# Splitting the pole transforms ahead of a spectral layer: half of the channels ahead, the rest in four parts inside the loop

## The chip, the core and the metric

The kernel runs on one core of a Trainium2 chip. Time is the device time of that core in microseconds (us). The engines are named as in the profile: PE is TensorE (matmul; PEld its weight loads), DVE is VectorE, ACT is ScalarE, POOL is GpSimd, and SP is the engine from whose queue most DMAs are issued. Each engine takes its instructions in a fixed order and waits on semaphores for the others. A smaller time is better.

## What is computed

The reference passes x of 16 x 16 x 256 x 256 through four residual layers, each `x = x + layer(group_norm(x))`: a 3x3 convolution written with FFTs, a filter of 5 taps on the diagonal, a Laplace layer with poles and residues, and a quantised 3x3 convolution. The change lies at the start of the third, layer 2:

```python
alpha = fft2(x)
A  = 1.0 / (omega1[:, None, None, None] - weights_pole1[None])   # [y, i, k, p]
Bm = 1.0 / (omega2[:, None, None, None] - weights_pole2[None])   # [x, i, k, q]
S = einsum('ikpq,oikp,xikq->oxik', weights_residue, A, Bm)
output_residue1 = einsum('biox,oxik->bkox', alpha, S)            # then ifft2
C = einsum('biox,oikp->bikpx', alpha, A)
D = einsum('bikpx,xikq->bikpq', C, Bm)
output_residue2 = einsum('bikpq,ikpq->bkpq', D, weights_residue)
```

There are 16 input channels i, 16 output channels k and 4 poles on each axis. C and D are not taken from alpha in the kernel: A and Bm are transformed back to the image domain once ("hats"), and then multiplied with x there.

## The kernel before

Layers 0 and 1 run together over the 16 samples and write their result to the DRAM tensors `x2d`. At their end the group statistics of the last sample come in, and then layer 2's first stage begins, in three pieces:

- *Tables.* `table(...)` loads constants: `y1`, `x1`, `x2`, `m1`, `m2`, `not0` to stay, and `full`, `nat`, `diag` for the pole transforms.
- *Pole transforms* (lines 699 to 731). For each axis m of two, the 1024 poles (16 channels of 64) are loaded, real part `pr` and imaginary part `pi`, each broadcast to all 128 partitions (L706, L707). For two halves o of the frequencies: `g = (pi - w)^2` and `e = pi - w` on ACT (L716, L717), `g + pr^2` and its reciprocal on DVE (L719), then `im = e g` on POOL, `nre = pr g` on DVE and `re = -nre` on ACT (L722). Sixteen pairs of matmuls with `full` then give `hats[m]` for all channels (L729), in groups that ACT copies out of PSUM (L731). An fp32 matmul appears as two records of PE in the profile. After this `rt`, the residues on a diagonal, is made (two products on DVE).
- *The loop*, 128 steps n: four groups of four samples, in each group eight pairs of channels, in each pair four samples b. `quarters` loads x and forms sums and differences (`u`, `qd`, on DVE and POOL). `forth` does, per channel, the transform along y and the product with `hats[0]` on PE (L766, L769) into one of three `ps_y` buffers, and ACT copies it out as `y` (L771). `across` does the transform along x (L780) into two of three `ps_a` buffers, ACT copies one (`pc`, L785), DVE makes `al` (L787, L788), and PE multiplies with `hats[1]` (L796), which DVE weighs with `rt` and POOL sums. `project` runs for each sample at the end of its channels (L813). Channels 8 to 15 of the hats are first needed at step n = 16, channels 12 to 15 at n = 24.

Beside the loop runs side work for the next stage, the generator `aside`: `sums_over_q` (L577 to L630), then `poles(0)` and `masked(0, 0)`. It is cut into 56 pieces, and `next(aside, None)` at the end of a step emits one.

Order: inside the loop PE is in the order in which the code is written (`manual_schedule` of PE alone). The order of the other engines, and all orders ahead of the loop, are set by a scheduler, so that side work can stand well ahead of the step in which it is written. The tiles of the pole transforms lie in the pool `tp`, which is given back before the loop; the pool `head` holds `af0`, `af1` and `l00` to `l11`, which `poles` and `masked` use later.

## Time and profile before

| | us |
|---|---|
| median of 3 runs (4469.8 to 4476.33) | 4475.6 |
| the profiled execution | 4466.67 |
| its span | 4464.9 |
| first table load for layer 2 issued | 1283.41 |
| first matmul of the loop (L766) | 1367.24 |
| last copy of y in the loop (L771), start | 2250.0 |

Times inside the span count from its start. PE is busy 89% of the span, PEld 69%, DVE 68%, ACT 62%, POOL 49%. In a timeline row the first number is the start, the second the length of the merged instructions, and what stands in brackets is the idle time of the engine before it and what ended that. In a row by groups the numbers after the count are the busy time and the mean nanoseconds of one instruction, then the idle time before. In a row by stretch each engine has its busy time and its number of instructions, and the last three columns are the granted PE clock (1.00 is full), the busy share of the DMA engines and GB/s.

### The profile page before, as it was taken

Reading aid. Unit: us, or ns where it says so; the run is one execution under the profiler, and the core shown is the slowest. Engines: PE = TensorE matmul, PEld = TensorE weight load, DVE = VectorE, ACT = ScalarE, POOL = GpSimd, SP = SyncE. Lnnn points to the kernel's source line nnn. Section 1 sums busy time; section 2 is a strip of 40 time slices with the busy share of each in tenths; the row PEclk is TensorE's granted clock in tenths of the full one; section 3 lists DMA queues with packets and bytes.
Section 4 is the critical chain, followed back from the end, with each engine's and each line's share of the span. In section 5 each row is a group of like instructions: output and inputs, shape, how many; then the busy total and the mean of one; then the engine's idle time right before and its main releaser. Section 6 shows DMA issues by size and latency. Waiting matters only on the chain. (4 is left out here: it accounts for less than half of the span.)

```text
span 4464.9 us, 122570 instructions
## 1 busy us (share of the span) xinstructions
PE 3986.4 (89%) x50800; PEld 3069.6 (69%) x50800; DVE 3051.8 (68%) x5654; ACT 2752.2 (62%) x3667; POOL 2208.0 (49%) x3466
## 2 busy tenths in 40 slices
PE   4999999999948999899989999997999999995776
PEld 1555555555527999899967777775778888883444
DVE  4767676767677878787755555554566666767998
ACT  2877777777623444444458888887544444445998
POOL 2242424232345546464556666664677777773222
PEclk9999999999978999999989999998999999997999
DMA  6777776767443545354447777777887878876998
GB/s 144 166 174 168 168 174 163 179 158 183 105 113 103 164 136 172 123 162 153 152 101 166 164 170 166 167 172 173 219 219 219 219 217 230 235 205 240 350 351 310
DMA packets 431340, 820.54 MB, mean 184 GB/s; under 512 B 41600, under 2 KB 306816, under 8 KB 415360
## 3 DMA queue, kind: packets, MB, share of 16 engines
q1 hardware_dynamic: 365248, 577.52, 50.2%
q0 software_dynamic: 65536, 235.18, 16.8%
q8 instruction: 401, 6.57, 0.7%
q14 instruction: 155, 1.27, 0.1%
HBM read 408.85 MB, written 336.07 MB: 167 GB/s over the span
## 5 line engine op out<-in xcount | busy, mean ns | idle before, releaser
L382 PE MATMUL ps<-va,wt 128*64 128x512 f32 (+1 forms) x1632 | 668.9, 571 | 11.4 <-POOL va L354 9.2
L382 PE MATMUL ps<-vb,wt 128*64 128x512 f32 (+1 forms) x1632 | 667.1, 570 | 4.6 <-DMA vb<-va 4.6
L878 ACT COPY sk<-ps_s 64x516 f32<-64x516 f32 x1016 | 593.0, 584 | 117.8 <-PE ps_s L873 98.5
L771 ACT ACTIVATE y<-ps_y,bc 128x384 f32<-128x384 f32 x512 | 297.1, 581 | 423.1 <-PE ps_y L769 423.1
L873 PE MATMUL ps_s<-t,l 128*128 128x258 f32 x2048 | 523.5, 398 | 18.7 <-ACT sk L878 8.1
L190 DVE TENSOR_TENSOR ob<-ps_m,other 128x256 f32<-128x256 f32 x512 | 271.1, 607 | 355.5 <-ACT other L966 350.8
L403 ACT ACTIVATE v<-xt,nm 32x2048 f32<-32x2048 f32 x248 | 497.2, 2005 | 9.8 <-PE ps L417 3.5
L417 PE MATMUL ps<-v,w1s 128*64 128x259 f32 x4096 | 481.8, 395 | 11.0 <-DVE v L401 6.7
L382 PEld LDWEIGHTS ps<-va,wt 128*64 128x64 f32 x1632 | 223.3, 137 | 311.3 <-issue 282.8
L873 PEld LDWEIGHTS ps_s<-t,l 128*128 128x128 f32 x2048 | 372.2, 192 | 93.5 <-ACT sk L878 8.4
L417 PEld LDWEIGHTS ps<-v,w1s 128*64 128x64 f32 x4096 | 337.2, 141 | 133.0 <-issue 24.1
L1079 PE MATMUL ps_o<-exp,fs 128*128 128x128 f32 x2048 | 402.7, 279 | 14.2 <-ACT fs L1125 14.2
L1078 PE MATMUL ps_o<-c_last,zt 128*128 128x128 f32 x2048 | 401.7, 278 | 0.2
L1218 PE MATMUL ps_c<-q,wt 64*64 64x512 bf16 (+1 forms) x4608 | 288.1, 401 | 105.2 <-ACT o L1265 88.1
L1078 PEld LDWEIGHTS ps_o<-c_last,zt 128*128 128x128 f32 x2048 | 327.1, 195 | 63.1 <-issue 62.5
L941 PEld LDWEIGHTS ps_m<-z,sk 128*32 128x32 f32 x16384 | 254.5, 110 | 129.3 <-issue 108.3
L941 PE MATMUL ps_m<-z,sk 128*32 128x64 f32 x16384 | 303.7, 222 | 38.6 <-issue 35.3
L190 POOL TENSOR_TENSOR acc<-acc,prod 128x256 f32<-128x256 f32 x240 | 228.2, 951 | 216.0 <-DVE prod L190 209.3
L190 POOL TENSOR_TENSOR w<-rq 128x512 f32<-128x512 f32 x256 | 320.9, 1280 | 26.2 <-ACT rq L1080 15.4
L1079 PEld LDWEIGHTS ps_o<-exp,fs 128*128 128x128 f32 x2048 | 317.0, 195 | 15.4 <-ACT fs L1125 15.4
L1218 PEld LDWEIGHTS <-wt 64*64 64x64 bf16 x4800 | 179.8, 113 | 213.8 <-issue 144.7
L766 PE MATMUL ps_y<-c_y,qd 128*128 128x128 f32 x2048 | 315.9, 277 | 5.1 <-ACT y L771 5.1
(347 smaller groups left out, 8853.0 us busy)
## 6 DMA issues: line engine op xcount, KB each, us to landing
xt<-x2d SPq DMA_DIRECT2D x256, 512.0 KB, 4.3
z<-alphad SPq DMA_DIRECT2D x516, 129.0 KB, 4.8
xt<-in_x_dram SPq DMA_DIRECT2D x256, 256.0 KB, 7.2
x2d<-x2s POOLq DMA_DIRECT2D x256, 256.0 KB, 5.0
mixd<-ob SPq DMA_DIRECT2D x128, 512.0 KB, 5.8
ot<-mixd SPq DMA_DIRECT2D x256, 256.0 KB, 7.2
x3d<-xt POOLq DMA_DIRECT2D x128, 512.0 KB, 5.7
xt<-x3d SPq DMA_DIRECT2D x64, 1024.0 KB, 8.8
```

The lines of the kernel that those rows point to most:

```text
L190: eng.tensor_tensor(o, a, b, op)
L382: nc.tensor.matmul(ps[halves[h], lo:hi, :], lhsT=wt0[:, w, :], rhs=v[:, 2 * t + lo : 2 * t + hi, j : j + N], start=j == 0 and k == 0, stop ...
L403: nc.scalar.activation(to, o.xt[c][q_], AF.Identity, bias=o.g.nm[q_, 1:2])
L417: nc.tensor.matmul(ps[halves[h], k, 0:U], lhsT=o.w1[:, w : w + 64], rhs=v1[:, lo : lo + U], start=first_, stop=not first_)
L766: nc.tensor.matmul(to[:, :, a, :], lhsT=v[:, c, a, i % 2, :], start=a == 0, stop=a == 1, rhs=y1[:, a].rearrange("p (r f) -> p r f", r=2))
L771: nc.scalar.activation(y[:, c, :], ps[:, 0 : 3 * P], AF.Copy, scale=bc2[:, b, i // 2, 0:1])
L873: nc.tensor.matmul(ps[:, d, 0 : 2 * NX], lhsT=ls[h][:, k + d - k0], rhs=t2[:, h, k + d].rearrange("p x r -> p (x r)"), start=True, stop=True)
L878: copy(sks[2 * e8 + n][64 * h : 64 * h + 64, :, 2 * k : 2 * k + 4] .rearrange("p x (k r) -> p x k r", r=2), ps[64 * n : 64 * n + 64, :, 0 ...
L941: nc.tensor.matmul(to, lhsT=sk[:, x_], rhs=z[:, :, x_], start=True, stop=True)
L1078: nc.tensor.matmul(ps[:, a, c, :], lhsT=zts[d][:, a, c, :], rhs=last[:, c, :], start=True, stop=False)
L1079: nc.tensor.matmul(ps[:, a, c, :], lhsT=fs[:, d, a, :], rhs=ey[:, d, c, :], start=False, stop=True)
L1218: nc.tensor.matmul(o, lhsT=wt[half[h], w, :], rhs=src, start=i == 0, stop=i == len(work[0]) - 1)
```

## The change

The pole transforms become a function `transforms(m, i0, ni, pool)` for `ni` channels from `i0`. It is called for channels 0 to 7 of both axes ahead of the loop, and four times inside it, for four channels each, after the matmuls of steps 2, 4, 8 and 10 (axis 0 and then axis 1 for channels 8 to 11, axis 1 and then axis 0 for channels 12 to 15). Inside the loop its tiles are those of `head`; `full` stays for the whole stage; the tile `cf` of the side work moves to `head`'s `af1`. e and g have one buffer each, where there was one for each half o. The side work begins at n = 17 in place of 9 and is dense from n = 61 in place of 81.

```diff
-        cf = new(pool, [HC * C, 4, NP], "cf")
+        cf = (new(head, [HC, 2, C, FC], "af1").rearrange("p h r k f -> p (h r k f)")
+              .rearrange("p (n m q) -> p n m q", m=4, q=NP))
...
-            full = table(tp, "full").rearrange("p (h m f) -> p h m f", m=2, h=2)
+            full = table(wp, "full").rearrange("p (h m f) -> p h m f", m=2, h=2)
             nat, diag = table(tp, "nat"), table(tp, "diag")
-            for m, (t, pole) in enumerate(((ty, p1b), (tx, p2b))):
+            ws = []
+            for m, t in enumerate((ty, tx)):
                 rs = over_step(tp, t, f"b{m}")
...
+            def transforms(m, i0, ni, pool):
+                pole, n = (p1b, p2b)[m], ni * KP
+                if pool:
+                    pr, pi, h, e, g = (pool.tile([P, n], F32, tag=k, name=f"{k}{m}") for k in ("pr", "pi", "h", "e", "g"))
+                    re, im, nre = (pool.tile([P, 2, n], F32, tag=k, name=f"{k}{m}") for k in ("re", "im", "nre"))
+                else:
+                    ts = [new(head, [2, n], k) for k in ("l00", "l10", "l01", "l11", "af0", "af1")]
+                    pr, pi, h, e, g = ts[0][:, 0], ts[0][:, 1], ts[1][:, 0], ts[1][:, 1], ts[2][:, 0]
+                    re, im, nre = ts[3:]
+                at = slice(i0 * KP, i0 * KP + n)
+                nc.sync.dma_start(pr, pole[0:1, at].to_broadcast([P, n]))
+                nc.sync.dma_start(pi, pole[1:2, at].to_broadcast([P, n]))
                 tt(Q, h, pr, pr, MUL)
                 for o in range(2):
-                    e, g = (tp.tile([P, C * KP], F32, tag=f"{k}{o}", name=f"{k}{m}{o}") for k in ("e", "g"))
-                    nc.scalar.activation(g, pi, AF.Square, bias=nw[:, o : o + 1])
-                    nc.scalar.activation(e, pi, AF.Identity, bias=nw[:, o : o + 1])
+                    nc.scalar.activation(g, pi, AF.Square, bias=ws[m][:, o : o + 1])
+                    nc.scalar.activation(e, pi, AF.Identity, bias=ws[m][:, o : o + 1])
                     tt(V, g, g, h, ADD)
                     V.reciprocal(g, g)
                     tt(Q, im[:, o, :], e, g, MUL)
                     tt(V, nre[:, o, :], pr, g, MUL)
                     nc.scalar.mul(re[:, o, :], nre[:, o, :], -1.0)
+                nb = min(ni, 8)
                 for o in range(2):
-                    for i in range(0, C, 8):
-                        cols = slice(i * KP, (i + 8) * KP)
+                    for i in range(0, ni, nb):
+                        cols = slice(i * KP, (i + nb) * KP)
                         for r, parts_ in enumerate(((re, im), (im, nre))):
                             ps = ps_y.tile([P, 8, KP], F32, tag="ps_y", name="ps_hat")
+                            to = ps[:, 0:nb]
...
-                            nc.scalar.copy(hats[m][:, o, i : i + 8, r, :], ps)
+                            nc.scalar.copy(hats[m][:, o, i0 + i : i0 + i + nb, r, :], to)
+
+            for m in range(2):
+                transforms(m, 0, 8, tp)
...
-            if n > 7 and (n % 2 or n > 80):
+            if n in (2, 4, 8, 10):
+                transforms(n // 2 % 2 ^ 1, 8 + 4 * (n > 7), 4, None)
+            if n > 15 and (n % 2 or n > 60):
                 next(aside, None)
```

More of the change, by code (lines that the diff above doesn't have):

```diff
@@ L698, in layers @@
             tp = tmp.enter_context(tc.tile_pool(name="b_t", bufs=1))
-            full = table(tp, "full").rearrange("p (h m f) -> p h m f", m=2, h=2)
+            full = table(wp, "full").rearrange("p (h m f) -> p h m f", m=2, h=2)
             nat, diag = table(tp, "nat"), table(tp, "diag")
-            for m, (t, pole) in enumerate(((ty, p1b), (tx, p2b))):
+            ws = []
+            for m, t in enumerate((ty, tx)):
                 rs = over_step(tp, t, f"b{m}")
-                w = tp.tile([P, 2], F32, tag=f"wn{m}", name=f"wn{m}")
+                w, nw = (wp.tile([P, 2], F32, tag=f"{k}{m}", name=f"{k}{m}") for k in ("wn", "nw"))
@@ L704, in layers @@
                 V.tensor_scalar(w, nat, rs, TWO_PI, MUL, MUL)
-                pr, pi, h = (tp.tile([P, C * KP], F32, tag=k, name=f"{k}{m}") for k in ("pr", "pi", "h"))
-                nc.sync.dma_start(pr, pole[0:1, :].to_broadcast([P, C * KP]))
-                nc.sync.dma_start(pi, pole[1:2, :].to_broadcast([P, C * KP]))
-                re, im, nre = (tp.tile([P, 2, C * KP], F32, tag=k, name=f"{k}{m}") for k in
-                               ("re", "im", "nre"))
-                nw = tp.tile([P, 2], F32, tag=f"nw{m}", name=f"nw{m}")
@@ L712, in layers @@
-                V.tensor_scalar(nw, w, -1.0, None, MUL)
+                V.tensor_scalar(nw, w, -1.0, None, MUL)
+                ws.append(nw)
+            def transforms(m, i0, ni, pool):
[10 more added lines that the diff above has]
+                nc.sync.dma_start(pi, pole[1:2, at].to_broadcast([P, n]))
@@ L722, in layers @@
                     nc.scalar.mul(re[:, o, :], nre[:, o, :], -1.0)
+                nb = min(ni, 8)
                 for o in range(2):
-                    for i in range(0, C, 8):
-                        cols = slice(i * KP, (i + 8) * KP)
+                    for i in range(0, ni, nb):
+                        cols = slice(i * KP, (i + nb) * KP)
                         for r, parts_ in enumerate(((re, im), (im, nre))):
                             ps = ps_y.tile([P, 8, KP], F32, tag="ps_y", name="ps_hat")
+                            to = ps[:, 0:nb]
                             for k, v_ in enumerate(parts_):
-                                nc.tensor.matmul(ps.rearrange("p i k -> p (i k)"), lhsT=full[:, o, k],
+                                nc.tensor.matmul(to.rearrange("p i k -> p (i k)"), lhsT=full[:, o, k],
                                                  rhs=v_[:, o, cols], start=k == 0, stop=k == 1)
-                            nc.scalar.copy(hats[m][:, o, i : i + 8, r, :], ps)
+                            nc.scalar.copy(hats[m][:, o, i0 + i : i0 + i + nb, r, :], to)
+            for m in range(2):
+                transforms(m, 0, 8, tp)
             res = tp.tile([P, 2, C, NP], F32, tag="res", name="res")
```

## The prediction

> **What bounds the kernel now.** I read the page first, then busy time by stretch around the place of the change, then the waits and the timeline of that place, and last the loop that follows it.

> ```profile
> span 4464.9 us, 122570 instructions
> PE 3986.4 (89%) x50800; PEld 3069.6 (69%) x50800; DVE 3051.8 (68%) x5654; ACT 2752.2 (62%) x3667; POOL 2208.0 (49%) x3466
> ```

> TensorE (PE) fills 89% of the span, so a gain has to come from a place where it stands still. Busy time by stretch (columns: stretch, length, busy time and instructions of each engine, granted clock, DMA):

> ```profile
> 1292.00:1313.00 21.00, 0.16 (x1) 0.16 (x1) 17.58 (x16) 6.62 (x7) 6.29 (x3) 0.50 0.62 182
> 1313.00:1330.00 17.00, 16.09 (x31) 6.85 (x32) 17.00 (x9) 7.90 (x11) 9.97 (x5) 0.84 0.29 93
> 1330.00:1351.00 21.00, 0.95 (x3) 0.15 (x1) 21.00 (x9) 1.64 (x2) 6.83 (x4) 0.63 0.18 50
> 1351.00:1367.00 16.00, 16.00 (x32) 6.97 (x33) 5.57 (x6) 5.16 (x8) 2.51 (x2) 0.84 0.21 66
> 1427.00:1477.00 50.00, 50.00 (x450) 50.00 (x449) 39.22 (x74) 22.80 (x49) 28.50 (x29) 1.00 0.53 170
> ```

> Between layer 1 and the loop of layer 2 the third number, VectorE (DVE), is full (17 of 17, 21 of 21) while PE has nothing or runs pole transforms. In the loop (last row) PE is full and DVE has 10.8 of 50 us free. The timeline of that place (start, length, engine, line, operation):

> ```profile
> 1283.41 0.35 SPq L186 DMA_DIRECT2D c_mod<-in_const_dram  x1
> ...
> 1297.34 1.22 DVE L190 TENSOR_TENSOR g<-g,h 128x1024 f32<-128x1024 f32 x1
> ...
> 1300.81 6.54 DVE L719 RECIPROCAL g<-g 128x1024 f32<-128x1024 f32 x1
> ...
> 1308.35 3.35 DVE L190 TENSOR_TENSOR nre<-pr,g 128x1024 f32<-128x1024 f32 x1
> ...
> 1348.49 4.44 DVE L190 TENSOR_TENSOR nre<-pr,g 128x1024 f32<-128x1024 f32 x2
> 1350.85 2.07 PE L729 MATMUL ps_hat<-re,c_full 128*128 128x512 f32 x2 [20.05 <-ACT re L722]
> ...
> 1367.24 0.61 PE L766 MATMUL ps_y<-c_y,qd 128*128 128x128 f32 x4
> ```

> The chain is: tables and poles load, DVE works from 1297.3 to 1352.9, PE does the last 32 transform records, and at 1367.24 the loop begins. Then the loop itself; first the copies of y, which are four in a step, so 32 are eight steps, then two of its instructions with the idle time before them, a sum of waits, and a row of the side work:

> ```profile
> 1368.20:1426.70 58.50, 18.50 (x32) 0.94 0.35 107
> 1426.70:1476.80 50.10, 18.61 (x32) 1.00 0.53 169
> ```
> ```profile
> 1389.64 0.63 ACT L604 ACTIVATE qg<-qe 128x516 f32<-128x516 f32 x1 [8.39 <-POOL qe L190]
> 1390.79 1.22 PE L766 MATMUL ps_y<-c_y,qd 128*128 128x128 f32 x4 [5.07 <-ACT y L771]
> ```
> ```profile
> PE ps_a L780 <- DVE al L788: 10.3, 9, 2.5
> L607 DVE RECIPROCAL qg<-qg 128x516 f32<-128x516 f32 x8 | 27.0, 3378 | 16.9 <-POOL qg L190 16.9
> ```

> A step takes 50.1/8 = 6.26 us, all PE. The first eight take 58.5; step 0 lacks one `across` (1.34, from its first record at 1370.70 to the next matmul at 1372.04), so they are 58.5 - 48.7 = 9.8 over. About 8 of it is one PE wait of 5.07, because ScalarE (ACT) stood 8.39 us at a Square of the side work with the copies of y queued behind it, and slow records in the step after (9.11 us from copy to copy, 2.85 over).

> **The change, part by part.** Each part is costed against the profiled execution (4466.67 us, 8.9 under the median of the runs, 4475.6). 0.2%, about what a measurement of this kernel can tell from no change, is 9 us.

> (1) *The stretch ahead.* DVE from the first addition to the last nre: 1352.93 - 1297.34 = 55.6 us without idle time. Four reciprocals are 26.2; the other 29.4 are four additions, four nre and two rt of 1024, four u and four qd of 512, or 28 units of 512, 1.05 us each. In the DVE order of the changed program the same stretch holds 24 units (additions 4, nre 4, rt 4, u 4, qd 6, and four half units of part 1, which the scheduler puts ahead), four reciprocals of 512 at 3.35 (6.54 for 1024, 3.378 for 516) and two of 256 at 1.75 (a reciprocal of that width in the loop): 24 x 1.05 + 13.4 + 3.5 = 42.1. One us is added for e and g, now single buffers, which makes ACT wait for the product that read them. The second pole load, which waits for the last nre of the first pole, is hidden: landing (3.66 us for 512 KB in the trace, less for half) and h take about 4 us, and the DVE has 6.5 us of other work before it needs them. If it is late, that is 2 us.

> The start moves too: the first poles are issued two places earlier (0.47 us each) with half the bytes (pr and pi landed 1.32 us apart, so 0.66 less for each), and the Square takes 0.64 instead of 1.15: 2.7 us. The last nre ends at 1294.6 + 43.1 = 1337.7.

> After it come re (0.64) and the eight PE records of the second half. Their price hangs on the clock. The trace has the first records after 20.05 us of idle time 0.85 us apart and, about 4 us later, 0.43; after 0.91 us of idle time they stayed at 0.43, and after the 5.07 in the loop they were slow. The idle time before these eight will be about 3.1 us (DVE work between the two nre: 1.75 + 1.05 + 0.5 + 3.35 + 1.05 + 1.05 = 8.75, less 5.6 for the eight records of the first half), between what the trace shows. [...] I take 3.4 and keep 2.2 more in the range. The loop then starts at 1337.7 + 4.1 = 1341.8, **25.4 us earlier**. With units at 0.68 (a product of 516 without a collision in the loop) it would be 34; with the eight additions and nre at 1.68 (half the 3.35 above, beside im on GpSimd), 20.

> (2) *The same matmuls, now in the loop.* Four parts of eight products of 256 columns, two records each: 64 records at half of 0.43 = **13.75 us** on a PE that is full. Nothing hides this.

> (3) *Waits that the parts add.* A part is two additions (0.4), two reciprocals (1.75) and two nre (0.5 to 0.85) on DVE, about 5.7 us; parts 2 to 4, less the first reciprocal of part 2, are 15 us. DVE has 1.35 us free per step, 16 in twelve steps, and the 13.75 of (2) besides, so the sum fits, but the bursts delay al, and PE has three ps_a. The nearest row is the side work's burst of the same kind: 10.3 us of PE wait over eight of them, 1.3 each. ACT gets ten instructions of 0.37 per part and holds the three ps_y a little longer. Four parts: **+5** (ends 0 and 15). GpSimd (POOL) gets h and two im per part, 12 of 0.6 to 0.95, in a queue that is idle 43% of the time. SP issues eight more loads, 3.8 us; the loads of xt queued behind them run two steps or more ahead, and no wait for xt shows in the loop. If that cover goes, one xt landing is 4.3 us. Costed at nothing.

> (4) *The early loss.* In the changed ACT order the side work's first Square stands before the first copy of y, and its POOL operand has nothing long ahead of it. The 9.8 us fall away, but the first copy of y waits about 1 us behind that Square: **-8.8** (ends 0 and -9.8).

> (5) *Side work.* Its 56 pieces came on odd n from 9 and on every n from 81 to 100; now on odd n from 17 and on every n from 61 to 94. Work is equal, but the dense stretch now crosses the group end at n = 63, where PE waits for `project` (7.1 us at the longest): **+2** (ends 0 and 7). The moved tables and cf replace loads and buffers one for one: nothing.

> Sum: -25.4 + 13.75 + 5 - 8.8 + 2 = **-13.5**: 4453.2 for a profiled execution like this one, 4462.1 for the median.

> **The rivals.**
> - *Flat.* The loads of parts 3 and 4 land late, and ACT stands at their Squares, each of which is queued between two copies of y, as it stood at the side work's. Two such holds are 2 x 5.07 plus 2 x 2.85 for the slow records = 15.8, in place of 5: -13.5 + 10.8 = -2.7, 4472.9. For it: one tile serves all parts, so a load waits for the part before. Against: PE asks four steps later.
> - *Slower.* PE comes to each part's matmuls, which stand in its order, before re and im are there. Four waits of 5.07 + 2.85 are 31.7 in place of 5: +13.2, 4488.8. It decides from (13.5 + 5)/4 = 4.6 us per part. For it: the parts run one after the other through the same tiles. Against: part 1 is computed before the loop starts, and parts 3 and 4 have two steps and more, 12.5 us, for a chain of some 12.
> - *Better.* DVE and POOL collide less with shorter pieces (0.68 per unit): -22, 4453.6.
> - *It doesn't do what it says.* The scheduler might have put all parts ahead; the order shows part 1 and one reciprocal of part 2 there, and they are in the sum.

> **How the numbers follow.** Main case 0.62, of which 0.08 ends within 9 us; better 0.08; flat 0.22; slower 0.08. Faster by over 0.2%: 0.54 + 0.08 = 0.62; within: 0.30; slower: 0.08. The range leaves out the slower case and the tail of the better one, and allows for the 6 us by which runs differ: 4453 to 4474.

> **What would show it.** Right: the first L781 matmul near 1342; eight copies of hat of 512 ahead of it and sixteen of 256 after; the first 16 steps about 10 us longer than the 108.6 (58.5 + 50.1) of before; PE waits at hat matmuls in the loop under 2 us. Wrong: an ACT Square of a part with a wait of 5 us or more, slow records after it, or a loop start after 1350.

## The result, and the profile after

| | before | after |
|---|---|---|
| median, us | 4471.68 (20 runs, 4457.53 to 4481.98) | 4457.14 (20 runs, 4448.65 to 4471.05) |
| ratio of the times, 95% interval | | 0.9969 (0.996 to 0.9979) |
| profiled execution; its span | 4466.67; 4464.9 | 4456.3; 4454.5 |
| table `mod` issued to the loop's first matmul | 83.8 | 58.4 |
| table `mod` issued to the last copy of y in the loop | 966.6 | 955.4 |

The ratio is 13.9 us of the 4471.68 (interval 9.4 to 17.9); the prediction had 13.5. The two traces stand 1.1 us apart already where the table `mod` is loaded (1283.41 and 1282.29), which both issue as the group statistics of the last sample end. That lies ahead of what the change saves, so I count from that DMA. The page of the changed kernel begins:

```profile
span 4454.5 us, 122713 instructions
PE 3987.7 (90%) x50832; PEld 3072.2 (69%) x50832; DVE 3051.0 (68%) x5678; ACT 2753.8 (62%) x3699; POOL 2210.3 (50%) x3478
```

PE has 1.3 us more to do and the span is 10.4 shorter: idle time went. Busy time by stretch around the place of the change (columns: stretch, length, busy time and instructions of PE, PEld, DVE, ACT and POOL, granted clock, DMA share, GB/s):

```profile
1296.00:1303.00 7.00, 0.00 (x0) 0.00 (x0) 7.00 (x5) 1.22 (x3) 4.70 (x4) 0.50 0.66 201
1320.60:1326.30 5.70, 0.00 (x0) 0.00 (x0) 5.70 (x4) 2.98 (x7) 1.26 (x1) 0.72 0.05 7
1427.00:1460.00 33.00, 30.77 (x273) 30.39 (x272) 27.50 (x43) 13.81 (x29) 28.15 (x31) 1.00 0.46 147
```

As before, DVE is full ahead of the loop (7.00 of 7, 5.70 of 5.70) while PE has nothing, only for a shorter time. In the loop (last row) PE has 2 us without work in 33. The timeline of the stretch:

```profile
1282.29 0.33 SPq L186 DMA_DIRECT2D c_mod<-in_const_dram  x1
...
1294.47 0.69 DVE L190 TENSOR_TENSOR g<-g,h 128x512 f32<-128x512 f32 x1 [3.13 <-ACT g L726]
...
1296.21 3.35 DVE L729 RECIPROCAL g<-g 128x512 f32<-128x512 f32 x1
...
1332.35 1.10 DVE L190 TENSOR_TENSOR nre<-pr,g 128x512 f32<-128x512 f32 x1
...
1334.44 1.13 PE L741 MATMUL ps_hat<-re,c_full 128*128 128x512 f32 x2 [2.63 <-ACT re L732]
1336.29 3.32 PE L741 MATMUL ps_hat<-im,c_full 128*128 128x512 f32 x4 [0.73 <-POOL im L190]
...
1340.67 0.61 PE L781 MATMUL ps_y<-c_y,qd 128*128 128x128 f32 x4
```

DVE's stretch runs from 1294.47 to 1333.45 (39.0 us, where it was 55.6), then come the last eight records of the transforms, and the loop's first matmul stands at 1340.67 (before: 1367.24). In the loop, the copies of y in the first eight steps and in the next eight (32 each), and two instructions of ACT with the idle time before them:

```profile
1342.70:1400.50 57.80, 17.83 (x32) 1.00 0.32 101
1400.50:1460.20 59.70, 18.45 (x32) 1.00 0.48 154
```
```profile
1342.23 0.63 ACT L606 ACTIVATE qg<-qe 128x516 f32<-128x516 f32 x1 [0.77 <-POOL qe L190]
...
1381.51 0.51 ACT L727 ACTIVATE l<-l,nw 128x256 f32<-128x256 f32 x1 [4.15 <-POOL af L190]
```

Where 58.5 and 50.1 us stood, there are 57.8 and 59.7, both at full clock. The Square of the side work (L606) waits 0.77 us and stands ahead of the first copy of y; before it waited 8.39 among them. Why it waited so long shows in the loads of the side work, which start with the table `c_turn`; first before the change, then after it:

```profile
1367.48 0.35 SPq L186 DMA_DIRECT2D c_turn<-in_const_dram  x1
```
```profile
1294.85 0.43 SPq L186 DMA_DIRECT2D c_turn<-in_const_dram  x1
```

Before, it was issued 84.1 us behind `mod`, 0.2 us after the loop's first matmul, where the tiles of the pole transforms had just been read for the last time; now it is issued 12.6 us behind `mod`. The longest hold of ACT is now at an Identity of a part (L727), which waits for the product on POOL that reads the one tile `e`. What PE waits for in these 16 steps is short (a row has what PE waited for, in all, times, longest; left out are 0.9 us for `prod` on DVE and 0.4 for y on ACT), and none of it stands at the matmuls of a part:

```profile
PE ps_a L795 <- DVE al L803: 1.5, 2, 1.4
PE ps_y L781 <- ACT hat L743: 1.4, 1, 1.4
```

### The profile page after: what moved, and what is told of

Read it like the earlier page. It is cut to its first block, busy times and chain, and to the rows that moved or that the text cites. A ratio compares the mean times of both kernels' runs of the same rounds, so it can differ in the third digit from the quotient of the medians.

```text
span 4454.5 us, 122713 instructions
## 1 busy us (share of the span) xinstructions
PE 3987.7 (90%) x50832; PEld 3072.2 (69%) x50832; DVE 3051.0 (68%) x5678; ACT 2753.8 (62%) x3699; POOL 2210.3 (50%) x3478
## 5 line engine op out<-in xcount | busy, mean ns | idle before, releaser
L382 PE MATMUL ps<-va,wt 128*64 128x512 f32 (+1 forms) x1632 | 670.2, 572 | 11.4 <-POOL va L354 9.2
L190 DVE TENSOR_TENSOR ob<-ps_m,other 128x256 f32<-128x256 f32 x512 | 271.0, 607 | 349.8 <-ACT other L984 345.6
L891 PEld LDWEIGHTS ps_s<-t,l 128*128 128x128 f32 x2048 | 371.4, 191 | 96.4 <-ACT sk L896 10.8
L190 POOL TENSOR_TENSOR acc<-acc,prod 128x256 f32<-128x256 f32 x240 | 231.0, 963 | 222.0 <-DVE prod L190 215.4
L190 POOL TENSOR_TENSOR w<-rq 128x512 f32<-128x512 f32 x256 | 320.8, 1280 | 26.2 <-ACT rq L1098 15.4
L781 PE MATMUL ps_y<-c_y,qd 128*128 128x128 f32 x2048 | 314.8, 277 | 1.4 <-ACT hat L743 1.4
```

Of the source, the lines that this page charges most:

```text
L190: eng.tensor_tensor(o, a, b, op)
L382: nc.tensor.matmul(ps[halves[h], lo:hi, :], lhsT=wt0[:, w, :], rhs=v[:, 2 * t + lo : 2 * t + hi, j : j + N], start=j == 0 and k == 0, stop ...
L781: nc.tensor.matmul(to[:, :, a, :], lhsT=v[:, c, a, i % 2, :], start=a == 0, stop=a == 1, rhs=y1[:, a].rearrange("p (r f) -> p r f", r=2))
L891: nc.tensor.matmul(ps[:, d, 0 : 2 * NX], lhsT=ls[h][:, k + d - k0], rhs=t2[:, h, k + d].rearrange("p x r -> p (x r)"), start=True, stop=True)
```

## The experiments

Each is compared with the kernel before, run on the same chip. The kernel before had medians of 4466.9 to 4473.3 there, so I compare ratios, in us of 4471.7. Profiled executions differ from each other by up to 18 us in the part after the loop (2208.8 to 2227.0), whose code no kernel here alters. A term of the sum is therefore read in the loop of the trace, and the total in the ratio. The columns of the traces: "start" is from the table `mod` to the first copy of y, then the length of steps 0 to 15 and of steps 16 to 126, and "end" is from the table to the last copy of y.

| kernel | ratio (95%) | us | start | steps 0-15 | steps 16-126 | end |
|---|---|---|---|---|---|---|
| before | | | 84.9 | 108.5 | 769.5 | 966.6 |
| changed | 0.9969 (0.996-0.9979) | -13.9 | 60.5 | 117.6 | 773.4 | 955.4 |
| changed, again | 0.9969 (0.9957-0.998) | -13.9 | 60.3 | 117.7 | 771.7 | 953.7 |
| old density of side work | 0.9994 (0.9981-1.0008) | -2.7 | 60.7 | 117.6 | 777.9 | 960.2 |
| before, new side work | 1.0006 (0.9995-1.0017) | +2.7 | 82.7 | 109.3 | 771.3 | 967.0 |
| no parts | 0.9928 (0.9914-0.9942) | -32.2 | 58.1 | 98.8 | 771.9 | 932.7 |
| all parts ahead | 1.0026 (1.0016-1.0037) | +11.6 | 95.4 | 98.8 | 772.1 | 970.3 |
| second e | 0.9967 (0.9953-0.9982) | -14.8 | 60.6 | 115.9 | 773.4 | 953.8 |
| parts close together | 0.9986 (0.9975-0.9996) | -6.3 | 59.4 | 120.9 | 772.6 | 956.9 |
| four channels ahead | 0.9958 (0.9943-0.9974) | -18.8 | 36.3 | 138.5 | 771.7 | 950.5 |
| the same, second e | 0.9953 (0.9936-0.9971) | -21.0 | 34.8 | 134.5 | 772.9 | 946.2 |
| the same, parts spread | 0.995 (0.9932-0.9968) | -22.4 | 36.3 | 126.4 | 772.9 | 939.4 |
| the same, with a pad | 0.9954 (0.9939-0.9969) | -20.6 | 43.0 | 128.1 | 771.1 | 946.2 |
| spread, re on POOL | 0.9945 (0.9928-0.9961) | -24.6 | 34.6 | 129.5 | 771.3 | 939.4 |

### The changed kernel again

> The changed kernel again, without an edit, on the chip of the next three, to compare them with. Theory: its loop starts 60.5 us after the load of the table mod is issued (1342.8 - 1282.29), its first 16 steps take 117.5 us, and the ratio to the kernel before is 0.9969 as in the result, or between 0.996 and 0.998. Rival: the gain hangs on the chip (the kernel before was at 4471.7 beside it and at 4467.3 beside the first four experiments); then the ratio is 0.998 to 0.9995.

The ratio came out at 0.9969 again, beside another measurement of the kernel before (median 4468.0 where it was 4471.7), and the first 16 steps within 0.2 us. The rival falls. Steps 16 to 126 took 771.7 us where the first trace had 773.4, so a difference of 2 us in that column is the spread between executions.

### The price of the parts: leave them out

```diff
+        for m in range(2):
+            for o in range(2):
+                Q.memset(hats[m][:, o, 8:], 0.5)
...
-            if n in (2, 4, 8, 10):
-                transforms(n // 2 % 2 ^ 1, 8 + 4 * (n > 7), 4, None)
```

> The changed kernel without the four parts inside the loop: the transforms of channels 8 to 15 are left out, and a constant is written there ahead of the loop. It prices the parts. Theory: the loop starts 6 us earlier (part 1 is worked ahead: two reciprocals of 1.74 and 2.65 of products on DVE), the first 16 steps fall from 117.5 to about 99.5 us (13.75 of matmuls and 4 of waits), and the time is 24 us below the changed kernel (about 4433). Rival: PE has idle time in these steps in any case and the parts' matmuls fill it in part; then the first 16 steps fall by 10 or less, and the time is 10 to 16 us below the changed kernel (4441 to 4447).

The copies of y, the first eight steps and the next eight:

```profile
1340.90:1389.70 48.80, 18.59 (x32) 1.00 0.37 120
1389.70:1439.70 50.00, 18.60 (x32) 1.00 0.53 170
```

98.8 us where 99.5 was expected: with the parts it was 117.6, so the four parts cost 18.8 us together. The rival (PE's idle time takes part of them in) falls. These rows show a second thing: the first eight steps have no loss at all (48.8 = 8 x 6.26 less 1.3), where the kernel before lost 9.7. The start was misjudged: 2.4 us earlier instead of 6. DVE does other work of the loop in that place, and then stands 1.57 us for a Square, which ACT reaches late, behind an Identity that waits for the product on POOL to free the one tile `e`. The total is 18.3 us below the changed kernel by the ratios (21 to 23 at the end of the loop in the traces), not 24.

### All parts ahead

```diff
             for m in range(2):
                 transforms(m, 0, 8, tp)
+            for m, i0 in ((0, 8), (1, 8), (1, 12), (0, 12)):
+                transforms(m, i0, 4, None)
...
-            if n in (2, 4, 8, 10):
-                transforms(n // 2 % 2 ^ 1, 8 + 4 * (n > 7), 4, None)
```

> The changed kernel with the four parts called ahead of the loop, right after the first half, with the same small tiles; nothing of the transforms is in the loop. Theory: what helps is that the loop starts before the second half of the channels is done. Three parts run one after the other through the same tiles, 8 to 9 us each, so the loop starts at about 1368 as before (26 us later than in the changed kernel), the first 16 steps lack 17.8 us, and the kernel is 6 to 12 us slower than the changed one (4463 to 4469). Rival: the gain comes from smaller pieces and shorter products ahead of the loop, not from the place; then it is as fast as the changed kernel or faster (4457 or less).

PE in the timeline, at the first half of parts 2, 3 and 4, the merged matmuls with the idle time before them, and the loop's first:

```profile
1347.23 1.22 PE L742 MATMUL ps_hat<-l,c_full 128*128 128x256 f32 x2 [5.86 <-ACT l L733]
...
1361.41 1.22 PE L742 MATMUL ps_hat<-l,c_full 128*128 128x256 f32 x2 [4.73 <-ACT l L733]
...
1372.91 1.22 PE L742 MATMUL ps_hat<-l,c_full 128*128 128x256 f32 x2 [5.26 <-ACT l L733]
...
1379.08 0.61 PE L784 MATMUL ps_y<-c_y,qd 128*128 128x128 f32 x4
```

The direction was right and the size was not: a part takes 12.6 us by itself (37.7 for three, from 1341.4, where part 1's matmuls end, to 1379.1), not 8 to 9, so the loop starts 34.9 us later than in the changed kernel, and the kernel is slower than the one before (by 3.7 us at the end of the loop, by 11.6 in the ratio). Smaller pieces one after the other through the same tiles gain nothing, then. What gains in the start is that the chain of load, Square, sum, reciprocal, product, negation and matmul, 12.6 us for a part, runs beside steps of the loop. The first 16 steps are 98.8 here as well. All transforms stand ahead of this loop, as before, and still the early loss is gone, because the Square of the side work stands ahead of the copies of y in the ACT order. Its table `c_turn` is issued 20.3 us behind `mod` here. So this part of the gain does not need parts in the loop.

### The kernel before with the new side work alone

```diff
-            if n > 7 and (n % 2 or n > 80):
+            if n > 15 and (n % 2 or n > 60):
```

> The kernel before with one edit: the side work begins at n = 17 and is dense from n = 61, as in the changed kernel; the pole transforms stay ahead. Theory: the later gate does not take away the early loss, because the first Square of the side work keeps its place among the first copies of y in the ACT order; the first eight steps stay at about 58 us, and the denser side work costs 2 to 4 us: 4474 to 4476 against 4471.7. Rival: the early loss went away in the changed kernel because the side work was moved later; then the first eight steps fall to about 49 us and the kernel is 5 to 7 us faster than before (about 4466).

```profile
1390.35 0.63 ACT L604 ACTIVATE qg<-qe 128x516 f32<-128x516 f32 x1 [9.72 <-POOL qe L190]
```

The Square keeps its place, behind ten copies of y, and waits 9.72 us; `c_turn` is issued 81.8 us behind `mod`, as late as before; the first eight steps take 59.2. The early loss does not go with the later start of the side work, as the theory said and the rival did not. Steps 16 to 126 take 771.3 in place of 769.5. The ratio gives +2.7 us with an interval from -2 to +8.

### The changed kernel with the old density

```diff
-            if n > 15 and (n % 2 or n > 60):
+            if n > 15 and (n % 2 or n > 80):
```

> The changed kernel with one edit: the side work is dense from n = 81 again (its 56 pieces end at n = 104), everything else stays. Theory: the steps 16 to 127 grew from 769.5 to 773.4 us because 34 pieces come one per step where 20 did; with the old density they return to about 769.5, and the kernel is 2 to 4 us faster than the changed one (4453 to 4455). Rival: those 3.9 us are the spread between executions and have nothing to do with the side work; then the time stays at 4457 within 2 us and the stretch at 773.

Both fall: it is slower than the changed kernel, by 11 us between the ratios, and steps 16 to 126 grow to 777.9. Steps 81 to 99 take 139.8 where the changed kernel has 130.1 (they hold the group end at n = 95, now beside one piece per step), and steps 64 to 80 take 120.2 where it has 128.1; the other steps add 2.7. So 4.5 of the 11 us are found in the loop. The rest is not placed; this trace is of the slowest of the twelve runs and its part after the loop is the longest of all (2227.0). The times scatter widely (4452.7 to 4478.0), and the medians of the same runs are only 6 to 8 us apart (6.7 below the kernel before, where the changed kernel has 12.6 and 14.5).

### A second tile for e

```diff
                 for o in range(2):
+                    if not pool:
+                        e = ts[1 + o][:, 1]
```

(The free half belongs to the tile `l01`, not to `af0` as the expectation has it.)

> The changed kernel with a tile of its own for the second e of a part (the free second half of af0), so that ACT's Identity needn't wait for the product on POOL that reads the first. Theory: the waits of the parts (4 to 5 us in the first 16 steps) come in part from ACT standing at that Identity (4.15, 1.97 and 0.86 us in the trace) with the copies of y queued behind it; the Identities wait no more, the first 16 steps fall from 117.5 to 115 or 116, and the time is 2 us below the changed kernel. Rival: the copies of y wait for PE in any case, and the waits of PE are those for al and hat; then nothing changes (117 to 118, the same time within 1.5 us).

ACT's waits in the stretch from 1335 to 1475, first the changed kernel run again, then with the second tile:

```profile
ACT l L728 <- POOL af L191: 7.0, 3, 4.6
```
```profile
ACT l L734 <- DVE af L190: 5.0, 3, 3.4
ACT l L728 <- POOL af L190: 0.2, 1, 0.2
```

The Identities waited 7.0 us for the product; with the second tile (there they are L729) they have no such row any more. The 0.2 us are at a Square (L728), which waits for the same product, and part of the wait comes back at the negation (L734). The first 16 steps fall by 1.8 us, as expected. The ratio cannot tell 2 us from nothing.

### The slower rival made to happen: parts in successive steps

```diff
-            if n in (2, 4, 8, 10):
-                transforms(n // 2 % 2 ^ 1, 8 + 4 * (n > 7), 4, None)
+            if n in (2, 3, 4, 5):
+                transforms((0, 1, 1, 0)[n - 2], 8 + 4 * (n > 3), 4, None)
```

> The changed kernel with its four parts after steps 2, 3, 4 and 5 in place of 2, 4, 8 and 10. It is the prediction's slower rival made to happen: PE comes to the matmuls of parts 2 to 4 after 6.3 + 3.5 us, and in the kernel with all parts ahead one such chain took 12.6 us. Theory: PE waits 3 to 6 us at each of three parts, and slow records follow; the first 16 steps take 127 to 137 us in place of 117.5, and the kernel is 10 to 20 us slower than the changed one (about the kernel before, or slower). Rival: the chain of a part was long there only because DVE and POOL had other work, and is 8 us or less here; then the time is that of the changed kernel within 3 us.

```profile
PE ps_hat L741 <- ACT l L732: 5.2, 3, 4.5
```

Now PE does wait at the matmuls of parts, 5.2 us over three waits, and the records after the 4.5 are slow (the first two take 1.22 us and the next six 2.77, where those of the half part before took 0.70 and 1.46; the granted clock from 1348 to 1419 is 0.95). But the first 16 steps grow by only 3.3 us, between rival and theory. The end of the loop is 1.5 to 3.2 us later than in the two traces of the changed kernel; the ratio gives 7.6 more. It remains faster than the kernel before. With parts in successive steps the mechanism costs far less than the 7.9 us per part that the prediction gave it.

### Four channels ahead, six parts

```diff
-                transforms(m, 0, 8, tp)
+                transforms(m, 0, 4, tp)
...
-            if n in (2, 4, 8, 10):
-                transforms(n // 2 % 2 ^ 1, 8 + 4 * (n > 7), 4, None)
+            if n in (2, 4, 6, 8, 10, 12):
+                transforms(*((0, 4), (1, 4), (0, 8), (1, 8), (1, 12), (0, 12))[n // 2 - 1], 4, None)
```

> The changed kernel with channels 0 to 3 ahead and six parts of four channels after steps 2, 4, 6, 8, 10 and 12. It moves the same boundary further. Theory: DVE ahead of the loop loses four reciprocals of 3.35 for four of 1.75 (6.4) and eight units at 0.92 halved (3.7), the last eight records halve (3), so the loop starts 13 us earlier; 6.9 us of matmuls and 2.5 of waits come in: 3 to 4 us below the changed kernel. Rival: six parts close together fill DVE (34 us of bursts against 37 free) and hold al; the first 16 steps grow by 20 and more, and the kernel is 5 to 10 us slower than the changed one.

The total is about what was expected (5 us below the changed kernel by the ratios, whose intervals overlap), but out of two terms that were both wrong. The start is 24 us earlier, not 13, and the first 16 steps grow by 20.9, not 9.4. From the timeline, and ACT's longest wait:

```profile
1242.99 0.43 SPq L722 DMA_DIRECT2D pr<-in_p1b_dram  x1
...
1286.64 0.34 SPq L186 DMA_DIRECT2D c_mod<-in_const_dram  x1
...
1288.54 0.42 DVE L190 TENSOR_TENSOR g<-g,h 128x256 f32<-128x256 f32 x1
```
```profile
ACT l L727 <- POOL af L190: 18.5, 5, 7.8
```

The first poles are issued 43.7 us ahead of the table `mod` (in the changed kernel 5.8 behind it), so that the first addition comes 1.9 us after the table in place of 12.2. In the loop, ACT stands 18.5 us at Identities, with copies of y queued behind. Behind the longest, 7.8 us, PE waits 5.0 us, as it waited 5.07 behind the side work's Square in the kernel before, where the granted clock was 0.50 from 1390.2 to 1397.0.

### The same with the second e, and with the parts spread

```diff
-            if n in (2, 4, 6, 8, 10, 12):
-                transforms(*((0, 4), (1, 4), (0, 8), (1, 8), (1, 12), (0, 12))[n // 2 - 1], 4, None)
-            if n > 15 and (n % 2 or n > 60):
+            if n in (2, 5, 8, 11, 14, 17):
+                transforms(*((0, 4), (1, 4), (0, 8), (1, 8), (1, 12), (0, 12))[n // 3], 4, None)
+            if n > 18 and (n % 2 or n > 58):
```

> Four channels ahead and six parts, as in the run with that boundary, and a tile of its own for the second e of a part. Theory: with six parts ACT stood 18.5 us at the Identities that wait for the product on POOL, and the first 16 steps were 138.6 us where 117.7 (the control) + 6.9 of matmuls make 124.6; the second e takes the larger part of the 14 away: first 16 steps 128 to 132, 7 to 10 us below the run without it, ratio to the kernel before 0.9935 to 0.9945. Rival: DVE is full in these steps (six bursts of 5.7), and the Identities only showed it; then the first 16 steps stay above 135 and the ratio at 0.9955 or more.

> As the run with four channels ahead and two tiles for e, with the six parts three steps apart (after 2, 5, 8, 11, 14 and 17) and the side work from n = 19, dense from n = 59. Theory: what is left of the waits comes from parts that follow each other within two steps (12.5 us and the matmuls); with three steps (18.8) each part's chain fits, the first 20 steps hold 20.7 us of matmuls and 5 or less of waits (steps of 6.26: 125.2 less 1.3, so 145 to 150), and the ratio to the kernel before is 0.993 to 0.994. Rival: the waits belong to each part (its copies and Squares stand between the copies of y) wherever it is put; then the first 20 steps take 155 or more and the time is that of the run two steps apart.

With the second e the first 16 steps are 134.5, 4 us less, between theory and rival. Spread as well, the first 20 steps take 154.6, where the kernel two steps apart took 159.5: 30.8 us over the 123.8 of a loop without parts, of which 20.7 are matmuls. So 10 us of waits stay, 1.7 per part, nearly what the rival said. The longest hold of ACT in these steps, and the wait of PE behind it:

```profile
1360.30 0.51 ACT L728 ACTIVATE l<-l,nw 128x256 f32<-128x256 f32 x1 [4.22 <-DMA l<-in_p1b_dram]
...
1362.12 0.71 PE L783 MATMUL ps_y<-c_y,qd 128*128 128x128 f32 x4 [1.56 <-ACT y L788]
```

This is a Square of a part (L728) whose load landed late, the cause that the prediction's flat rival named. Such holds are 15.7 us in all here, five of them. PE's waits of over a microsecond follow them three times (1.6, 1.3 and 1.4 us), a negation once (1.2), and once the Square of the side work (2.0), which stands behind 11 copies of y again and waits 4.1 us. So not every wait belongs to a part. The loop ends 14 to 16 us earlier than in the changed kernel.

### Where the earlier start comes from: a pad

```diff
+            pad = tp.tile([P, 2816], F32, tag="pad", name="pad")
+            Q.memset(pad[:, 0:1], 0.0)
             ws = []
```

> The run with four channels ahead, two tiles for e and parts three steps apart, with an idle tile of 11 KB per partition put ahead of the transforms' tiles in their pool, so that these lie again where they lie in the changed kernel. Theory: with four channels ahead the loop began 24 us earlier, not the 13 expected, because the smaller pool no longer lies over tiles of layer 1 in use: its first poles were issued at 1243.0 instead of 1288.1, 43.7 us ahead of the table mod, and the first addition came 1.9 us after that table in place of 12.2. With the pad the poles are issued behind the table mod again, the loop starts 46 to 48 us after it in place of 36.3, and the kernel is 10 us slower than the same without the pad (4457 where that had 4446.7, ratio to the kernel before about 0.997). Rival: DVE is the limit ahead of the loop in any case and the early poles only let it idle; then the start moves by 3 us or less and the time stays.

```profile
1283.75 0.33 SPq L186 DMA_DIRECT2D c_mod<-in_const_dram  x1
...
1289.52 0.43 SPq L724 DMA_DIRECT2D pr<-in_p1b_dram  x1
...
1294.54 0.43 DVE L190 TENSOR_TENSOR g<-g,h 128x256 f32<-128x256 f32 x1 [1.74 <-ACT g L730]
```

With 11 KB that nobody uses, the poles are issued 5.8 us behind the table again and the first addition comes 10.8 after it. The start moves from 36.3 to 43.0 us (the loop's first matmul from 32.7 to 41.9) and the loop ends 6.7 later. So the size of the pool decides when the loads may go; over which tiles it lies is the theory's reading, and no trace shows it. It is worth 6.7 us at the end of the loop, not 10. The ratios (0.9950 and 0.9954) cannot tell 7 us apart.

### The negation on POOL

```diff
-                    nc.scalar.mul(re[:, o, :], nre[:, o, :], -1.0)
+                    if pool:
+                        nc.scalar.mul(re[:, o, :], nre[:, o, :], -1.0)
+                    else:
+                        Q.tensor_scalar(re[:, o, :], nre[:, o, :], -1.0, None, MUL)
```

> The same kernel without the pad, with the negation that makes re of a part on POOL in place of ACT. Theory: ACT stood 20.4 us at these negations (waiting for nre from DVE) with copies of y and hat queued behind, and the waits of PE for y (8 us in the first 20 steps) come from that; they fall to 3 or less, the first 20 steps from 154.7 to 149 or 150, and the ratio to the kernel before is 0.9935 to 0.9945. Rival: the negation on POOL lands later (its queue holds u and the sums of the products), PE waits at the matmuls of the parts instead, and nothing is gained or 3 us are lost.

PE's longest waits, first with the negation on ACT, then on POOL:

```profile
PE ps_y L783 <- ACT y L788: 4.7, 5, 1.6
```
```profile
PE ps_a L800 <- ACT y L791: 4.4, 3, 2.7
```

The wait changes its name and hardly its size. That fits the holds above: only one of the five waits followed a negation. The twelve negations now take 12.5 us on POOL, and PE's longest wait, 2.7 us, follows a Square of a part that stood 5.2 us for POOL. The first 20 steps take 158.0 (154.6 before the edit), the start is 1.7 earlier, and the loop ends at 939.4 in both. The rival holds as to the gain: none is seen in the loop. Its ratio, 0.9945, is the lowest of the complete kernels, and not told apart from the 0.9950 of the kernel without this edit. Both are faster than the changed kernel by some 8 to 11 us as the ratios stand, with intervals that touch or overlap, and by 14 to 16 us in the loops of the traces.

## Why the prediction was right, step by step

The total was right, and so were the paths of its three large terms. That it came within half a microsecond is partly luck, since errors inside the first term cancel and the reason given for the last was not confirmed.

- *(1) The start.* The first matmul of the loop comes 58.4 us after the table `mod`, before 83.8: 25.4 earlier, as predicted. Inside, three terms were off, by -4.1, +1.0 and +3.1 us, and cancelled; the exact hit is luck. The DVE stretch was sized at 43.1 us and took 39.0: the six reciprocals are the 16.9 of the sum, but the 24 units are 0.92 each and not 1.05 ((39.0 - 16.9) / 24), and the microsecond added for single buffers did not appear. Against this the first addition came 1.0 later after the table than assumed, and the tail of re and eight records took 7.2 in place of 4.1.
- *The tail and the clock.* The prediction took 3.4 us for the eight records, eight at 0.43. That they stay fast after some 3.1 us of idle time was assumed: no run shows it, and in this one they took 5.5 us, beside a wait of 0.73. (The row after 20.05 us of idle time was read short too: there the records went at 0.43 only 5.2 us later, so that eight take 6.1, not the 5.6 counted for the first half.) PE was idle for 2.63 us, the first two ran fast, then it waited 0.73 for `im` on POOL, which the prediction had not seen, and half a microsecond after that the granted clock fell from 1.00 to 0.50. In rows by stretch, the two stretches of 3.41 us before the fall and the one after it:

```profile
1329.97:1333.38 3.41, 1.84 (x5) 0.53 (x3) 3.41 (x4) 1.49 (x4) 1.63 (x2) 1.00 0.21 71
1333.38:1336.79 3.41, 1.62 (x3) 0.59 (x4) 3.41 (x4) 1.00 (x3) 3.41 (x3) 1.00 0.59 166
1336.79:1340.21 3.42, 3.42 (x5) 1.33 (x4) 3.42 (x8) 0.58 (x1) 0.86 (x1) 0.50 0.54 175
```

  In this trace the clock rises at 1306.1, 1319.7, 1330.0 and 1340.2, which lie 13.7, 10.2 and 10.2 us apart (4, 3 and 3 times 3.41), and falls at 1336.8, 3.4 before the last. PE worked 1.62 us in the 3.41 ahead of that fall. With all parts ahead, the same eight records came after 2.41 us of idle time, without a second wait, and took 3.5 us. The 2.2 us held in the range were the right order. They cost little in the end: in the second trace of the changed kernel, where the two waits were 1.8 and 1.0 us, the loop's first matmul came 1.9 us earlier, but the first copy of y, behind the Square, only 0.2.
- *(2) and (3) The parts in the loop.* Predicted 13.75 + 5 = 18.75; measured 18.8, the difference between the loops with and without them. Copies of hat 0.86 us apart, four in each part, are 13.8 us; 5.0 is left for waits. The prediction took the size from bursts on DVE; of the 4.2 us that PE waited, 2.4 were for DVE (`al`, `prod`) and 1.8 for ACT (`hat`, `y`), which stood up to 4.15 us at Identities behind a single `e`. The second tile took 1.8 us away.
- *(4) The early loss.* Predicted -8.8. The first 16 steps without parts are 9.7 shorter than before, and the first copy of y stands 2.1 us behind its matmul where it stood 1.1: -8.7. The reason was right too: with the new density alone in the kernel before, the Square kept its place and the loss stayed; with the Square ahead of the copies it was gone, even with all transforms ahead. What moved the Square lies one step back. `c_turn` is issued 84.1 and 81.8 us behind `mod` in the two kernels with the old, larger tiles of the transforms, and 11.6 to 26.8 in the twelve others. That the side work's tiles lay over those of the transforms would explain it, but no run tests this alone.
- *(5) The side work.* Predicted +2; 1.9 in the kernel before with the new side work alone, 2.2 and 3.9 in the two traces of the changed kernel. That is no more than executions differ, and with the old density the steps took longer, not shorter: the reason, the dense stretch across a group end, is not confirmed.
- *The sum* in the trace is -25.4 + 18.8 - 8.7 + 3.9 = -11.4, at the end of the loop it is -11.3 (966.6 to 955.4), and -12.9 in the second trace (953.7); the ratio has -13.9. Moving half of the transforms into the loop gave -25.4 + 18.8 = -6.6 of it; the larger share, -8.7, came with the place of one Square. Of the signs named, the first matmul near 1342 was at 1340.67, and the first 16 steps grew by 9.0 us for about 10. No PE wait stood at a part's matmuls in the loop.
- *The rivals.* "Flat" began to happen: Squares of parts waited for their loads, 2.7 us at the longest, but PE waited 1.4 us at most in these steps, and not there, and no slow record followed. With six parts it did happen in part. "Slower" needs parts in successive steps; even then it costs 3.3 us in the first 16 steps. "Better" is out: the units did not fall to 0.68. And the parts do stand in the loop, with sixteen copies of hat of 256.

Not settled: why the old density in the changed kernel costs 11 us by its ratio (6 to 8 by the medians) when its trace shows only 4.5 in the loop; and whether the early loss goes when the side work's tiles alone are moved.

## What to carry to other kernels

Preparation that chains several engines costs its whole length ahead of a loop when its pieces pass through one set of tiles (12.6 us for a part here; done in the old, longer pieces, the same four parts cost 25.4 us ahead, 6.4 each). Inside the loop it costs only what it takes of the full engine, plus a wait (3.4 and about 1.3 us for a part here). So move what the first steps don't need into the loop, until its price per part meets the time it takes ahead. Look at the order of the in-order engine that empties PSUM: one instruction of side work that waited among its copies cost 9.7 us here, and about 1 when it stood ahead of them; a single tile shared by two halves makes such a wait (4.15 us in the changed kernel), and so does a load that lands late (4.22 with the parts spread). Look at when the loads of side work are issued, too: here 84 us behind `mod` before the change and 13 after it, though the change does not touch them. The size of a pool ahead of a stage can hold its loads back: here 11 KB less moved the first load forward by 49 us and the start of the loop by 7.

## What was not expected of the hardware

The granted clock of PE fell from 1.00 to 0.50 half a microsecond into a busy stretch (at 1336.8), after two idle stretches of 2.63 and 0.73 us, and rose again 3.4 us later with PE busy all the time. With all parts ahead the same eight records came after 2.41 us of idle time alone and took 3.5 us, where they took 5.5 here. So in a chain of short bursts 2.41 us of idle time cost the records nothing, and 2.63 and 0.73 us cost them 2.
